# A 3x3 depthwise convolution folded into nine matmuls, or done as one projection matmul and multiply-adds on VectorE

## The chip, the cores and the metric

The kernel runs on one core of a Trainium2 chip. The metric is the device time of one execution in microseconds (us). Engines are named as the profile names them: PE is TensorE (PEld its weight loads), DVE is VectorE, ACT is ScalarE, POOL is GpSimd, SP is SyncE, which here only issues DMAs. ACT issues DMAs too, in order with its other work (ACTq in the profile).

## What is computed

The reference is a stack of four layers on an input of 4 images of 64 x 64 pixels and 96 channels. Layers 0 and 1 are selective scans over the image in four directions; layers 2 and 3 are a linear attention and a quantised feed-forward part. The change is in layers 0 and 1, in the step from the normalised input to the input of the scan:

```python
xz = jnp.einsum('bhwc,ec->bhwe', x, in_proj_w)          # 96 -> 2 x 192 channels
xx, z = jnp.split(xz, 2, axis=-1)
xc = jnp.transpose(xx, (0, 3, 1, 2))
xc = conv_general_dilated(xc, conv_w, (1, 1), [(1, 1), (1, 1)],
                          feature_group_count=E) + conv_b   # 3x3, each of 192 channels by itself
xc = silu(xc)
...
x_dbl = einsum('bkdl,kcd->bkcl', xs, x_proj_weight)     # xs: xc in four orders
delta = softplus(einsum('bkrl,kdr->bkdl', dts, dt_projs_weight) + bias)
... scan over 4096 positions, sum of the four directions, layer norm, * silu(z), out projection
```

x is normalised per group of 3 channels before this.

## The kernel before, in words

The work of layers 0 and 1 is four phases: each of two layers, for each of two pairs of images. `Scans.run` (L701) does for each phase first `prepare` and then `scan_phase`. Beside the `prepare` of a phase runs the `finish` of the phase before it; the last `finish` runs alone. After these come the token layers, which the change doesn't touch.

`prepare` (L151) and `finish` (L548) are Python generators. `run` takes one yield of `prepare` after another, adds the phase's number `beside` to an account at each, and lets `finish` go on by one yield for every full 1.0 in the account (L712). So `beside` says how many yields of `finish` are traced per yield of `prepare`. `finish` has 208 yields. Tracing gives an order of precedence; outside `scan_phase`, which is written under `manual_schedule`, the framework's planner then lays out each engine's queue: it takes, by its own estimate of when inputs and buffers are ready, the earliest traced instruction that is ready. On the chip each engine works through its queue in that fixed order and waits at the head of it. (In the trace, for example, the L277 copies of one half stand between the L270 activations of the other half, which come before them in the code.)

`prepare` does these things in turn:

- loads the small weights and takes the statistics of the two images (L186 to L209), which end in `gs`, the mean and scale per channel;
- loads `in_w` (96 x 192) and the nine taps, broadcast over 96 partitions, and multiplies them into `taps` (96 x 9 x 192) on DVE (L215): nine matrices that hold projection and convolution together;
- `convolve` of image 0 (L220) with `beside` 0.0;
- with `beside` 0.5, `steps` of image 0, 16 calls of 6 yields each with the two in `prepare` itself; in between, `convolve` of image 1 goes on by two yields per call (L228);
- with `beside` 1.7, `steps` of image 1, again 16 calls.

`convolve` (L234) holds the normalised image in `xn`, 66 x 66 with a border of zeros (one buffer). Eight loads of 192 KB on SP's queue (`rawi`, two buffers) bring it, each with every eighth row; DVE normalises each into its strided place (L248). Then, for each half of 96 of the 192 output channels and each of eight chunks of 512 pixels, nine fp32 matmuls accumulate in one of two PSUM banks of the pool `p_c` (L263; the profile shows each as two records), and ACT takes Silu of the bank into `xc` (L270). Last, 16 copies of `xc` scaled on ACT (L277, which reads every eighth float) go to DRAM by DMAs that ACT issues.

`steps` (L285) uses the same two banks. It makes, for a chunk in one direction and for the same chunk in reverse: matmuls (L292), two evacuations on ACT (L295, L296), matmuls (L309), then for each of the two Softplus on ACT (L317), a bf16 copy on ACT (L318), a product on DVE (L319), a difference on DVE (L320), a copy on POOL (L323), a difference on DVE (L324), and DMAs to DRAM that ACT and SP issue (L304, L322, L326). `delta`, `parts` and `du` have two buffers each.

`finish` works through four quarters of the images with single buffers, most of it as one chain over PE, ACT and DVE (L563 to L697), with its loads (`yk`, `ud_f`, `xs`) on SP's queue.

Of the kernel before, what the change touches and what calls it, by code (L numbers as in the profile page):

```python
# [9 lines left out]
F32 = mybir.dt.float32  # L10
# [3 lines left out]
AF = mybir.ActivationFunctionType  # L14
ALU = mybir.AluOpType
# [5 lines left out]
HW = 64  # L21
L = HW * HW
C = 96
E = 192
# [4 lines left out]
PAD = HW + 2  # L29
# [41 lines left out]
def view(t, off, *dims):  # L71

    return bass.AP(t.tensor, t.offset + off, [t.ap[0]] + [list(d) for d in dims])
# [57 lines left out]
class Scans:  # L131
# [19 lines left out]
    def prepare(self, ph):  # L151
# [16 lines left out]
        with self.tc.tile_pool(name="prep", bufs=1) as wp, self.tc.tile_pool(  # L168
# [25 lines left out]
            for i in range(2):  # L194
# [17 lines left out]
            taps = wp.tile([C, 9, E], F32, name="taps")  # L212
            nc.sync.dma_start(taps, a[pre + "conv_w"].unsqueeze(0).broadcast_to([C, 9, E]))

            nc.vector.tensor_tensor(  # L215
                taps, taps, in_w.unsqueeze(1).broadcast_to([C, 9, E]), ALU.mult
            )

            xc = [wp.tile([C, 2, L], F32, name="xc", bufs=2) for _ in range(2)]
            yield from self.convolve(ph, 0, x, xc[0], taps, conv_b, dsum)  # L220
            ph.beside = 0.5
            other = self.convolve(ph, 1, x, xc[1], taps, conv_b, dsum)
            for i in range(2):
                for c in range(NC):
                    for k in range(2):
                        yield from self.steps(ph, sp, xc[i], xp, dt_w, i, k, c)
                        for _ in range(2):
                            next(other, None)  # L228
                            yield
                for _ in other:  # L230
                    yield
                ph.beside = 1.7

    def convolve(self, ph, i, x, xc, taps, conv_b, dsum):  # L234
# [3 lines left out]
        with self.tc.tile_pool(name="conv", bufs=1) as cp:  # L238
            xn = cp.tile([C, PAD, PAD], F32, name="xn")
            for edge in (xn[:, 0, :], xn[:, PAD - 1, :], xn[:, 1 : PAD - 1, 0], xn[:, 1 : PAD - 1, PAD - 1]):  # L240
                nc.vector.memset(edge, 0.0)
            for hl in range(8):
                raw = cp.tile([C, 8, 8, 8], F32, name="rawi", bufs=2)
                nc.sync.dma_start(
                    raw.rearrange("c a h w -> c a (h w)"), x[:, hl * 8 : hl * 8 + 8, i]
                )
                yield
                nc.vector.tensor_scalar(  # L248
                    view(xn, (1 + hl) * PAD + 1, (1, 8), (8 * PAD, 8), (8, 8)),
                    raw,  # L250
                    ph.gs[:, i, 0:1],
                    ph.gs[:, i, 1:2],
                    ALU.subtract,
                    ALU.mult,
                )
            for h in range(2):
                for c in range(NC):
                    if c % 2 == 0:
                        yield
                    ps = self.bank()  # L260
                    for tap in range(9):
                        dy, dx = divmod(tap, 3)
                        nc.tensor.matmul(  # L263
                            rows(ps[:C]),
                            taps[:, tap, h * C : (h + 1) * C],
                            xn[:, ROWS * c + dy : ROWS * (c + 1) + dy, dx : dx + HW],
                            start=tap == 0,
                            stop=tap == 8,
                        )
                    nc.scalar.activation(  # L270
                        xc[:, h, c * TC : (c + 1) * TC], ps[:C], AF.Silu, bias=conv_b[:, h : h + 1]
                    )
            for h in range(2):
                for hl in range(8):
                    yield
# [656 lines left out]
def laid_out(i):  # L932
    x = i["x"].reshape(NP, 2, 8, 8, 8, 8, C)
    a = {"x": x.transpose(0, 6, 3, 5, 1, 2, 4).reshape(NP, C, HW, 2, 64)}
    for n, gamma, beta in (("L0_", "ln_gamma", "ln_beta"), ("L1_", "out_norm_g", "out_norm_b")):
        p = n + "conv_"
        a[n + "in_proj_w"] = i[p + "in_proj_w"].T
        a[n + "conv_w"] = i[p + "conv_w"].reshape(E, 9).T
# [52 lines left out]
```

## Time and profile before

| | us |
|---|---|
| median of 3 runs | 12245.72 |
| lowest and highest run | 12240.04, 12246.47 |
| profiled execution, its own time | 12191.39 |
| span of the profiled execution | 12189.6 |
| L263, the nine taps' matmuls, busy in all | 1033.2 |
| L270, Silu of the convolution, busy in all | 87.3 |
| L248, normalising, 64 instructions, median of one | 0.756 |
| L428, the scans on DVE, busy in all (two groups) | 6347.5 and 868.1 |

The profiled execution was some 54 us shorter than the median of the runs. The page gives, in its second part, the busy share of each engine in 40 slices of the span in tenths; in its fifth part, groups of instructions by line, with busy time, the mean of one and the idle time of the engine ahead of them, with what ended it. A table of stretches gives for each stretch of time the busy time of every engine and, in brackets, its number of instructions, then the granted PE clock as a share of full speed, the busy share of the DMA engines and GB/s.

### The profile page before, as it was taken

The page shows a single profiled execution, that of the slowest core. Times are in us where ns is not written, and L with a number is a line of the kernel's source. Part 1 is how long each engine was busy: PE and PEld are TensorE (multiplying, and loading weights), DVE is VectorE, ACT ScalarE, POOL GpSimd, SP SyncE. Part 2 cuts the span into 40 slices and gives each one's busy share as a digit, 9 for nine tenths or more (in the row PEclk, how much of TensorE's full clock was granted, in tenths as well). Part 3 has the DMA queues.
Part 4 walks back from the last instruction along what each step waited for, and adds up shares of the span by engine and source line. Part 5 has one row for each costly group of instructions (what it writes and reads, how often), then busy time and mean ns, then how long its engine had stood idle before and what let it go on. Part 6 is the DMA issues. An engine that isn't in the chain of part 4 may idle for free.

```text
span 12189.6 us, 340681 instructions
## 1 busy us (share of the span) xinstructions
PE 9338.7 (77%) x147008; PEld 4884.4 (40%) x147008; DVE 9363.7 (77%) x9235; ACT 7063.0 (58%) x11815; POOL 7391.0 (61%) x2316
## 2 busy tenths in 40 slices
PE   7757777769877777769877777768877777776777
PEld 2224444433334444433334444433334444444333
DVE  2479999963569999982569999982459999993667
ACT  2456666643456666653457666653447666662556
POOL 0159999950149999960139999970119999990000
PEclk8669999989779999989778998988778999998887
DMA  3577777744667777754567777764567777773110
GB/s 95 168 228 257 257 254 254 253 167 142 207 211 256 254 254 255 254 199 130 180 217 257 257 258 255 256 215 125 172 201 251 254 254 254 254 249 124 18 21 11
DMA packets 906195, 2491.48 MB, mean 204 GB/s; under 512 B 278030, under 2 KB 560756, under 8 KB 773236
## 3 DMA queue, kind: packets, MB, share of 16 engines
q1 hardware_dynamic: 578036, 2163.43, 52.2%
q10 hardware_dynamic: 326656, 306.25, 8.5%
q8 instruction: 1158, 18.97, 0.7%
q14 instruction: 345, 2.83, 0.1%
HBM read 1955.47 MB, written 513.80 MB: 203 GB/s over the span
## 4 chain that ended last, share of the span: by engine, by line
DMA 57%; PE 20%; SPq 9%; DVE 5%; ACT 4%; issue 3%; POOL 1%; ACTq 1%; DVEq 0%; POOLq 0%
DMA h<-du 52%; SPq L401 9%; PE c L263 8%; PE f L596 2%; PE d L309 2%; DMA yk<-y 1%; PE c L292 1%; DMA delta<-parts 1%; PE f L605 1%; PE f L687 1%; PE f L676 1%; POOL parts L323 1%; DVE parts L324 1%; PE f L662 1%; PE ph L806 1%
## 5 line engine op out<-in xcount | busy, mean ns | idle before, releaser
L411 POOL TENSOR_TENSOR h<-h,b 128x1536 f32<-128x1536 f32 x2048 | 7021.7, 3462 | 527.6 <-DMA h<-du 187.1
L428 DVE TENSOR_TENSOR_SCAN h<-a,carry,h 128x512 f32<-128x512 f32 x5376 | 6347.5, 1259 | 176.7 <-POOL h L411 174.0
L421 ACT ACTIVATE a<-a,a_col 128x512 f32<-128x512 f32 x6144 | 4035.0, 664 | 1869.5 <-PE a L417 1831.7
L446 PEld LDWEIGHTS y<-h,cw 128*32 128x32 f32 x131072 | 2785.2, 128 | 3513.8 <-issue 1328.8
L446 PE MATMUL y<-h,cw 128*32 128x48 f32 x131072 | 3658.5, 266 | 523.3 <-DVE h L428 217.4
L417 PE MATMUL a<-dlt,rep 72*128 72x512 bf16 x6144 | 2529.7, 422 | 1315.1 <-DVE h L428 1228.6
L323 POOL CAST parts<-dl 96x1024 bf16<-96x1024 f32 x256 | 341.2, 1348 | 3092.4 <-DVE dl L320 2708.9
L319 DVE TENSOR_TENSOR du_sb<-dl,xc 96x1024 f32<-96x1024 f32 x256 | 396.2, 1574 | 1292.5 <-ACT dl L317 1241.5
L458 ACT COPY d<-y 128x384 f32<-128x384 f32 x2048 | 979.8, 478 | 468.2 <-PE y L446 418.4
L263 PE MATMUL c<-xn,taps 96*96 96x512 f32 x2304 | 1033.2, 609 | 73.2 <-DVE xn L248 70.8
L428 DVE TENSOR_TENSOR_SCAN h<-a,h 128x512 f32<-128x512 f32 x768 | 868.1, 1200 | 167.5 <-DMA h<-du 69.3
L417 PEld LDWEIGHTS <-rep 72*128 72x128 bf16 x6144 | 486.4, 98 | 829.4 <-issue 566.5
L309 PE MATMUL d<-xd,dt_w 7*96 7x512 f32 x1024 | 518.2, 856 | 255.7 <-ACT xd L295 224.9
L263 PEld LDWEIGHTS c<-xn,taps 96*96 96x96 f32 x2304 | 382.8, 167 | 707.4 <-issue 629.2
L828 POOL MEMSET tn<- 1x4096 f32 x8 | 27.8, 3506 | 861.8 <-PE pa L848 511.9
L270 ACT ACTIVATE xc<-c,conv_b 96x512 f32<-96x512 f32 x128 | 87.3, 682 | 714.3 <-PE c L263 628.2
L596 PE MATMUL f<-yk,perm 128*128 128x384 f32 x1024 | 417.1, 547 | 94.9 <-DMA yk<-y 90.4
L324 DVE TENSOR_TENSOR parts<-dl,parts 96x1024 bf16<-96x1024 f32 x256 | 366.9, 1455 | 154.3 <-POOL parts L323 154.3
L317 ACT ACTIVATE dl<-d 96x1024 f32<-96x1024 f32 x256 | 251.9, 1017 | 392.5 <-DMA delta<-parts 228.2
L292 PE MATMUL c<-xc,x_proj 96*103 96x512 f32 x512 | 421.8, 961 | 4.2 <-ACT xc L270 4.2
L309 PEld LDWEIGHTS d<-xd,dt_w 7*96 7x96 f32 x1024 | 151.9, 212 | 544.6 <-ACT xd L295 296.8
L363 ACT ACTIVATE cw<-c,gmask 128x256 f32<-128x256 f32 x512 | 285.6, 569 | 118.4 <-DMA c<-bc 62.2
(114 smaller groups left out, 5641.4 us busy)
## 6 DMA issues: line engine op xcount, KB each, us to landing
h<-du SPq DMA_DIRECT2D x1024, 768.0 KB
h<-du SPq DMA_DIRECT2D x2048, 384.0 KB
delta<-parts ACTq DMA_DIRECT2D x512, 288.0 KB
dlt<-delta SPq DMA_DIRECT2D x512, 288.0 KB
du<-du_sb SPq DMA_DIRECT2D x256, 384.0 KB
du<-du_sb ACTq DMA_DIRECT2D x256, 384.0 KB
y<-d SPq DMA_DIRECT2D x2048, 48.0 KB
yk<-y SPq DMA_DIRECT2D x256, 384.0 KB
```

The lines of the kernel that those rows point to most:

```text
L263: nc.tensor.matmul(rows(ps[:C]), taps[:, tap, h * C : (h + 1) * C], xn[:, ROWS * c + dy : ROWS * (c + 1) + dy, dx : dx + HW], start=tap == ...
L292: nc.tensor.matmul(rows(ps[:XD2]), xp[:, k, h], u[:, h], start=h == 0, stop=h == 1)
L309: nc.tensor.matmul(ps[:, m], dt_w[part, k, m * C : (m + 1) * C], xd[part], start=True, stop=True)
L324: nc.vector.tensor_tensor(parts[:, 2], delta, parts[:, 1], ALU.subtract)
L401: self.nc.sync.dma_start(u.h[32 * first : 32 * (first + quarters), e : e + n].rearrange("p e t -> p (e t)"), source.rearrange("a g e t -> ...
L411: self.nc.gpsimd.tensor_tensor(h, h, b, ALU.mult)
L417: self.nc.tensor.matmul(u.a[n], self.cst.rep[:, h], u.dl[:, e], start=True, stop=True)
L421: self.nc.scalar.activation(u.a[n], u.a[n], AF.Exp, scale=u.ph.a_col[:, at : at + 1])
L428: self.nc.vector.tensor_tensor_scan(u.h[:, n], u.a.pop(n), u.h[:, n], 0.0 if u.c == 0 else u.ph.carry[:, at : at + 1], ALU.mult, ALU.add,)
L446: self.nc.tensor.matmul(view(u.y[32 * j : 32 * j + 32], l2 * EB, (8 * EB, 4), (1, EB)), u.ph.cw[u.c][:, l1, 8 * j + l2], view(u.h, 64 * l1 ...
L458: self.nc.scalar.copy(u.d[:, :, :, l1], u.y[:, : 32 * EB].rearrange("p (t h x) -> p t h x", t=4, h=2))
L596: nc.tensor.matmul(ps[:, : 4 * C].rearrange("p (w v e) -> p w v e", w=4, v=nv), cst.perm[:, k], view(t, off, (sw if k < 2 else -sw, 4), (1 ...
```

## The change

The projection is done by itself: for each half, eight matmuls with the 96 x 96 half of `in_w` as weights, each on 512 normalised pixels. ACT copies the result out of PSUM into `xp`, the projected half image with its border of zeros (one buffer, used first for one half and then for the other). The input is loaded and normalised once per half, so twice per image, now in place and dense; it is the ACT copy that writes with a stride. The convolution then runs on `xp`: for each chunk of 512 pixels, ACT writes tap 0 times the pixels into the chunk of `xc`, DVE adds the other eight taps with `scalar_tensor_tensor`, in place, each with a scalar per partition, and ACT takes Silu in place. The L277 copies of a half now follow that half.

The weights are no longer multiplied together; the taps are loaded as 96 x 2 x 9. The yields of `convolve` stay 32 per image, but lie otherwise: per half four in the projection, one for each of eight chunks, and four in the copies to DRAM. The numbers `beside` are 1.0 for the convolution of image 0 (with one yield more ahead of it), 0.6 for the steps of image 0 and 1.25 for those of image 1.

```diff
-            taps = wp.tile([C, 9, E], F32, name="taps")
-            nc.sync.dma_start(taps, a[pre + "conv_w"].unsqueeze(0).broadcast_to([C, 9, E]))
-
-            nc.vector.tensor_tensor(
-                taps, taps, in_w.unsqueeze(1).broadcast_to([C, 9, E]), ALU.mult
-            )
+            taps = load("conv_w", [C, 2, 9])
...
-            yield from self.convolve(ph, 0, x, xc[0], taps, conv_b, dsum)
-            ph.beside = 0.5
-            other = self.convolve(ph, 1, x, xc[1], taps, conv_b, dsum)
+            ph.beside = 1.0
+            yield
+            yield from self.convolve(ph, 0, x, xc[0], in_w, taps, conv_b, dsum)
+            ph.beside = 0.6
+            other = self.convolve(ph, 1, x, xc[1], in_w, taps, conv_b, dsum)
...
-                ph.beside = 1.7
+                ph.beside = 1.25
...
             for h in range(2):
+                xp = cp.tile([C, PAD, PAD], F32, name="xp")
+                for edge in (xp[:, 0, :], xp[:, PAD - 1, :], xp[:, 1 : PAD - 1, 0], xp[:, 1 : PAD - 1, PAD - 1]):
+                    nc.vector.memset(edge, 0.0)
+                for hl in range(8):
+                    raw = cp.tile([C, TC], F32, name="rawi", bufs=2)
+                    nc.sync.dma_start(
+                        raw.rearrange("c (a p) -> c a p", p=64), x[:, hl * 8 : hl * 8 + 8, i]
+                    )
+                    if hl % 2 == 0:
+                        yield
+                    nc.vector.tensor_scalar(
+                        raw, raw, ph.gs[:, i, 0:1], ph.gs[:, i, 1:2], ALU.subtract, ALU.mult
+                    )
+                    ps = self.bank()
+                    nc.tensor.matmul(
+                        ps[:C], in_w[:, h * C : (h + 1) * C], raw, start=True, stop=True
+                    )
+                    nc.scalar.copy(
+                        view(xp, (1 + hl) * PAD + 1, (1, 8), (8 * PAD, 8), (8, 8)),
+                        ps[:C].rearrange("c (a h w) -> c a h w", a=8, h=8),
+                    )
                 for c in range(NC):
-                    if c % 2 == 0:
-                        yield
-                    ps = self.bank()
+                    yield
+                    acc = xc[:, h, c * TC : (c + 1) * TC]
                     for tap in range(9):
                         dy, dx = divmod(tap, 3)
-                        nc.tensor.matmul(
-                            rows(ps[:C]),
-                            taps[:, tap, h * C : (h + 1) * C],
-                            xn[:, ROWS * c + dy : ROWS * (c + 1) + dy, dx : dx + HW],
-                            start=tap == 0,
-                            stop=tap == 8,
-                        )
-                    nc.scalar.activation(
-                        xc[:, h, c * TC : (c + 1) * TC], ps[:C], AF.Silu, bias=conv_b[:, h : h + 1]
-                    )
-            for h in range(2):
+                        src = xp[:, ROWS * c + dy : ROWS * (c + 1) + dy, dx : dx + HW]
+                        w = taps[:, h, tap : tap + 1]
+                        if tap == 0:
+                            nc.scalar.activation(rows(acc), src, AF.Copy, scale=w)
+                        else:
+                            nc.vector.scalar_tensor_tensor(
+                                rows(acc), src, w, rows(acc), ALU.mult, ALU.add
+                            )
+                    nc.scalar.activation(acc, acc, AF.Silu, bias=conv_b[:, h : h + 1])
                 for hl in range(8):
-                    yield
+                    if hl % 2 == 0:
+                        yield
```

More of the change, by code (lines that the diff above doesn't have):

```diff
@@ L231, in prepare, with convolve @@
                     yield
-                ph.beside = 1.7
-    def convolve(self, ph, i, x, xc, taps, conv_b, dsum):
+                ph.beside = 1.25
+    def convolve(self, ph, i, x, xc, in_w, taps, conv_b, dsum):
         nc = self.nc
         with self.tc.tile_pool(name="conv", bufs=1) as cp:
[L239 to L245, printed above, removed]
-                )
-                yield
[L248 to L254, printed above, removed]
-                )
-            for h in range(2):
+            for h in range(2):
+                xp = cp.tile([C, PAD, PAD], F32, name="xp")
[19 more added lines that the diff above has]
+                    )
@@ L257, in convolve @@
                 for c in range(NC):
-                    if c % 2 == 0:
-                        yield
-                    ps = self.bank()
+                    yield
+                    acc = xc[:, h, c * TC : (c + 1) * TC]
                     for tap in range(9):
                         dy, dx = divmod(tap, 3)
-                        nc.tensor.matmul(
-                            rows(ps[:C]),
-                            taps[:, tap, h * C : (h + 1) * C],
-                            xn[:, ROWS * c + dy : ROWS * (c + 1) + dy, dx : dx + HW],
-                            start=tap == 0,
-                            stop=tap == 8,
-                        )
@@ L270, in convolve @@
-                    nc.scalar.activation(
-                        xc[:, h, c * TC : (c + 1) * TC], ps[:C], AF.Silu, bias=conv_b[:, h : h + 1]
-                    )
-            for h in range(2):
+                        src = xp[:, ROWS * c + dy : ROWS * (c + 1) + dy, dx : dx + HW]
[6 more added lines that the diff above has]
+                            )
@@ L274, in convolve @@
+                    nc.scalar.activation(acc, acc, AF.Silu, bias=conv_b[:, h : h + 1])
                 for hl in range(8):
-                    yield
+                    if hl % 2 == 0:
+                        yield
                     xu = cp.tile([C, 8, 64], F32, name="xu", bufs=2)
@@ L937, in laid_out @@
         a[n + "in_proj_w"] = i[p + "in_proj_w"].T
-        a[n + "conv_w"] = i[p + "conv_w"].reshape(E, 9).T
+        a[n + "conv_w"] = i[p + "conv_w"].reshape(2, C, 9).transpose(1, 0, 2)
         a[n + "conv_b"] = i[p + "conv_b"].reshape(2, C).T
```

## The prediction

> **What bounds the kernel now.** I read the page first, then the busy time by stretch of the stages outside the scans, then the groups of instructions, the waits and the timelines inside one such stage. The page says that no engine is the bound over the span:
>
> ```profile
> PE 9338.7 (77%) x147008; PEld 4884.4 (40%) x147008; DVE 9363.7 (77%) x9235; ACT 7063.0 (58%) x11815; POOL 7391.0 (61%) x2316
> ...
> DVE  2479999963569999982569999982459999993667
> ```
>
> DVE stands at 9 tenths in four scan phases, which the change doesn't touch, and the dips between them are the four stages that prepare a scan. Only there can time move. Stretches of the first stage (no finish beside it) and of the second; the columns are length, then PE, PEld, DVE, ACT, POOL busy with counts, then PEclk, DMA share, GB/s:
>
> ```profile
> 40.00:178.00 138.00, 126.00 (x287) 47.63 (x288) 5.27 (x8) 20.43 (x24) 0.00 (x0) 1.00 0.10 20
> 178.00:490.00 312.00, 252.62 (x478) 83.62 (x476) 131.75 (x102) 129.96 (x139) 43.09 (x30) 0.74 0.53 152
> 490.00:738.00 248.00, 133.40 (x196) 42.87 (x196) 144.79 (x102) 93.44 (x105) 49.27 (x34) 0.50 0.68 202
> ...
> 2688.00:2816.00 128.00, 128.00 (x293) 48.31 (x293) 2.86 (x4) 21.38 (x25) 0.00 (x0) 0.98 0.08 17
> 2816.00:3140.00 324.00, 284.75 (x671) 111.83 (x670) 143.22 (x150) 147.29 (x170) 39.17 (x28) 0.82 0.59 179
> 3140.00:3525.00 385.00, 316.76 (x959) 166.41 (x958) 223.66 (x318) 180.42 (x236) 43.63 (x36) 0.73 0.65 203
> ```
>
> I call the three stretches A (convolution of image 0 alone), B (steps of image 0, with convolution 1 and some finish) and C (steps of image 1, with the rest of finish). A is PE alone at 100%, 128 us. B is PE at 88%. In C nothing is full. The groups of the second stage (busy, mean ns, idle before):
>
> ```profile
> L263 PE MATMUL c<-xn,taps 96*96 96x512 f32 x576 | 257.5, 607 | 17.9 <-DVE xn L248 17.9
> ...
> L319 DVE TENSOR_TENSOR du_sb<-dl,xc 96x1024 f32<-96x1024 f32 x64 | 99.4, 1576 | 304.2 <-ACT dl L317 287.5 <-DMA du<-du_sb 12.9 <-DMA bc<-xd 3.8
> ...
> L324 DVE TENSOR_TENSOR parts<-dl,parts 96x1024 bf16<-96x1024 f32 x64 | 88.8, 1406 | 41.5 <-POOL parts L323 41.5
> ...
> L277 ACT ACTIVATE xu<-xc,dsum 96x512 f32<-96x512 f32 x32 | 38.5, 1220 | 15.4 <-DMA delta<-parts 6.9 <-DMA ud<-xu 6.8 <-ACT xu L277 0.8
> ```
>
> Without convolution or finish (second image of the first stage) the steps are a serial loop over engines. The DVE timeline there:
>
> ```profile
> 545.62 2.35 DVE L319 TENSOR_TENSOR du_sb<-dl,xc 96x1024 f32<-96x1024 f32 x2 [4.66 <-ACT dl L317]
> 547.90 2.35 DVE L320 TENSOR_TENSOR dl<-dl,parts 96x1024 f32<-96x1024 f32 x2
> 551.18 3.16 DVE L324 TENSOR_TENSOR parts<-dl,parts 96x1024 bf16<-96x1024 f32 x2 [0.93 <-POOL parts L323]
> 559.02 1.92 DVE L319 TENSOR_TENSOR du_sb<-dl,xc 96x1024 f32<-96x1024 f32 x1 [4.68 <-ACT dl L317]
> ```
>
> L319 to L319 is 13.4 us here, and 14.8 for the piece before (530.85 to 545.62). One such round I call a piece, an image has 16: 226 us at this mean, 235 from the stretch of 248 without its first and last half pieces; I take 232 (236 in the first stage). DVE idles some 5.6 us in each, ahead of L319 and L324. Where convolution 1 runs on PE (2920 to 3050), the waits show it standing before the steps, up to 31.3 us at once:
>
> ```profile
> PEld c L263 <- issue: 67.2, 239, 0.8
> DVE du_sb L319 <- ACT dl L317: 61.1, 4, 31.3
> ```
>
> [...] two-input L119 at 96x512 took 677 to 690 ns. [...] table loads took 1283. [...] L324 took 1187 ns at least and up to 2027, beside L323. [...] L277 reads every eighth float and took 1220.
>
> **The change part by part**, for one stage of two images.
>
> PE: 576 records of L263 go (257.5 us); 64 of the same size come (257.5/576 = 0.447, so 28.6). Net -229 us.
>
> DVE: 256 multiply-adds come. The nearest row is L119, 0.684; theirs has a pointer scalar, and the one-column form with one (L203, 215 ns) against the one without (L118, 154) gives 60 ns more: 0.744 us, so 190 us. Bounds: 0.68 without the pointer's price; above, [...] 0.84 for one collision (L324's 2027 less 1187), and GpSimd has 32 casts beside each image's steps, so up to 27 us more. Normalising goes from 16 at 0.753 to 32 dense ones at about 0.54 (L654): 12 to 17. Four memsets become eight per image, 112 ns each: +0.9. The taps product (1.96) goes. Net about +194 us: 97 an image, up to 124 with every collision.
>
> ACT: [...] 32 evacuations with a strided write, between L683's dense 0.582 and L277's strided read 1.22, I take 1.0[...]. Together +55 us. One chunk per yield where there were two can add Silu/Softplus switches: up to 8 pairs of 1.28, 0 to 20 us.
>
> DMA: 16 more loads of 192 KB on SP's queue, 3 MB a stage, 15 us at the 203 GB/s of C; they sit in that queue before finish's yk and xs loads and the steps' du, and each waits for its buffer until a matmul has read it. Hidden by DVE's multiply-adds, except before the first tap. The 648 KB taps load goes.
>
> A. Every tap needs all eight projections, since each covers every eighth row. Loads came in rounds of two, about 3 us (L248 at 2689.6, then 2692.9); now the matmul and the copy add about 1.5: 4 rounds, 18 us. Then 64 x 0.744 = 48 us, then, with one xp buffer, about 15 us of projection before the second half, then 48 us. That is 130 us, against 138 in the first stage and 128 in the second. So A doesn't shrink: DVE takes PE's place. It is 0 in the first stage and I take +10 in the others, where 33 of finish's 208 yields now stand beside it (the last finish, which runs alone, has 107 us of DVE; 33/208 of that is 17, partly in the gaps).
>
> C. Finish has 208 yields; the factor 0.5 over B's 96 yields lets 48 go by, so C has 160. (385-232)/160 = 0.96 us a yield. Now the factors are 1.0 over A's 33 and 0.6 over B's 96, so 208-33-58 = 117 remain: 232 + 112 = 344, so -41.
>
> B. Steps 232, finish 58 x 0.96 = 56, and the part of convolution 1 that isn't hidden. Before, it was 324-232-46 = 46 of 129 on PE, in the first stage 312-236 = 76. DVE has 288-132-30 = 126 us of slack beside steps (half of L319, L320 and L324's 265) and finish (58/208 of 107), and convolution 1 asks for 97 to 124. As DVE serves its queue in order, an L319 behind multiply-adds waits, and ACT's queue now holds a Silu that waits for eight multiply-adds, with Softplus L317 behind it, for which L319 waits. Bounds: nothing exposed, or all 124. I take half of that, 62: the loop's idle is in four places a piece and the multiply-adds come in two bursts. B = 232+56+62 = 350, +26; in the first stage 236+62 = 298, -14.
>
> Sum: 3 x (10+26-41) - 14 = -29 us. Against the profiled execution, 12191.4 (span 12189.6 and 1.8 around it), this makes 12162. That execution lies 54 us under the runs' median; the difference carried to the median gives 12217.
>
> **The rivals.**
> *DVE and ACT lock step (slower).* Place: B. The multiply-adds of two chunks, 16 x 0.744 = 12 us, meet a loop with 5.6 us of slack, and ACT, with 147 us busy and 5.2 us of DMA issue a piece (L322, L326 and L304 in its timeline; 83 us), gets 28 to 48 more. For it: every DVE operation of the loop is on its path. Against: only 8 of B's 16 pieces get multiply-adds. If 105 instead of 62 is exposed in each of the four stages, that is +172, so +143: 12389. It is slower than before from about 69 exposed.
> *PE was the drag (faster).* PE is 82% busy in C and 88% in B. If C follows PE's load (43 of finish's 208 yields leave it, 55 of its 267 us of PE, so 262 of 317 remain: 318 us, -67) and B exposes only a quarter of 124 (31, so 319, -5; first stage -45): 3 x (10-5-67) - 45 = -231: 12015. For it: the 31.3 us wait. Against: the loop alone, in the first stage's C, leaves PE half idle and takes its 232 all the same.
> *The change doesn't move the stages*, because the planner's order hides either work: 12246. Little speaks for it, A being fully exposed.
>
> **How the numbers follow.** Forecast 0.50 (spread some 60 us either way), lock step 0.30, PE drag 0.18, no movement 0.02. 0.2% is 24 us, about what a measurement of this kernel tells from no change. Faster by more: 0.25 of the forecast's 0.50 and 0.18, 0.43. Within: 0.15 + 0.02 = 0.17. Slower: 0.10 + 0.30 = 0.40. Both signs are likely; the forecast's own range is 12140 to 12295. The whole one goes to 12050, which leaves out over half of the fast rival (0.11), and to 12430, which leaves out a third of lock step (0.09), where all 124 and some table loads are exposed.
>
> **What would show it.** A: DVE over 70% busy in a stretch of 125 to 145 us, PE under 45%. Multiply-adds of 0.72 to 0.78 us[...]. B near 350 us: over 390 is lock step, with waits of L317 behind Silu and of Silu for DVE; under 325 is PE drag. C near 344. The prediction is wrong if A itself grows past 150 us, through gaps before each half, or if finish is left over after C.

## The result and the profile after

The changed kernel took 12214.17 us (median of 19 runs) against 12240.04 us of the kernel before (19 runs beside it): a ratio of 0.9981, 95% interval 0.9973 to 0.9990. So it is some 23 us faster, at the edge of what this kernel's measurement can tell. The forecast of 12217 us is met. But its parts, one for each stretch of a stage, are not: all three failed and their errors cancelled, which is what this study is about.

The page after, its lines of busy time and of DVE's slices:

```profile
PE 8693.3 (71%) x144960; PEld 4628.3 (38%) x144960; DVE 10072.3 (82%) x10351; ACT 7378.4 (60%) x12140; POOL 7390.2 (60%) x2316
...
DVE  6679999987669999987669999997559999993667
```

PE is down by 645 us over the span, DVE up by 709, ACT up by 315. In the dips between the scan phases DVE's slices of 2 to 6 tenths have become 5 to 8. The work went over to DVE, as announced, and the time hardly moved.

The profiled executions can't be subtracted as they stand: their spans are 12189.6 us before and 12223.4 after, because the four scan phases, whose code is the same, took 44 us more in the second one (7466 against 7421 us; a phase lay anywhere between 1836 and 1878 us in the profiles of this study). I therefore measure each stage alone, from the end of the last scan to the first one of the next phase. A ends with the 16th Silu of the convolution, B with the 32nd L323 (L324 before), C with the 64th. The time for statistics and small weights, some 40 us, is in A here. Each kernel's stages are read from one profiled execution. Its three later stages, which do the same work, differ among themselves by up to 2.6 us in A, 9 in B and 10 in C, so a difference of a few us between two means says little in B or C.

| us | A | B | C | whole stage |
|---|---|---|---|---|
| before, first stage | 179.5 | 330.6 | 228.1 | 774.0 |
| after, first stage | 169.3 | 331.2 | 234.4 | 771.0 |
| before, mean of the other three | 188.4 | 358.7 | 349.4 | 930.7 |
| after, mean of the other three | 187.5 | 362.7 | 341.2 | 926.7 |

The four stages sum to 3566 us before and 3551 after: 15 us less, of which A gives 13, C 18, and B and the way to the scan take 16 back. The stretches of the second stage (A, B, C) before, in the columns of the prediction's table:

```profile
2625.60:2814.90 189.30, 135.15 (x554) 55.22 (x555) 26.15 (x53) 29.97 (x39) 0.00 (x0) 0.84 0.19 46
2814.90:3171.30 356.40, 308.96 (x727) 122.83 (x725) 160.83 (x163) 163.38 (x187) 44.96 (x32) 0.80 0.58 177
3171.30:3518.10 346.80, 293.65 (x904) 155.91 (x904) 206.01 (x305) 165.40 (x219) 37.84 (x32) 0.75 0.66 208
```

and after, with B and C of the first stage ahead of them:

```profile
169.30:500.50 331.20, 158.34 (x220) 44.68 (x220) 229.05 (x248) 168.41 (x179) 43.02 (x32) 0.58 0.56 158
500.50:734.90 234.40, 124.76 (x184) 40.19 (x184) 135.78 (x96) 89.41 (x100) 46.43 (x32) 0.50 0.69 200
2641.70:2829.10 187.40, 86.31 (x492) 46.23 (x492) 123.11 (x224) 76.50 (x101) 0.00 (x0) 0.67 0.40 113
2829.10:3192.20 363.10, 231.59 (x468) 96.03 (x468) 253.77 (x326) 192.44 (x219) 45.42 (x32) 0.59 0.59 169
3192.20:3533.20 341.00, 260.30 (x712) 130.65 (x712) 191.38 (x252) 168.14 (x208) 38.01 (x32) 0.70 0.62 187
```

B went from PE at 87% to PE at 64% and DVE at 70%, and it is no shorter. Two things are to be seen against the prediction. B ends at 3171 in the profile before, not at 3140, where I had cut it. And the first stage's B is 331 us in both kernels, to within 1 us. The groups after, over the whole second stage:

```profile
L268 DVE SCALAR_TENSOR_TENSOR xc<-xp,conv_w,xc 96x512 f32<-96x512 f32 x256 | 176.5, 746 | 4.9 <-ACT xc L266 3.5 <-ACT xp L254 0.4
L308 PE MATMUL d<-xd,dt_w 7*96 7x512 f32 x256 | 141.7, 926 | 54.3 <-ACT xd L294 49.5 <-ACT xd L295 4.7
L251 PE MATMUL c<-rawi,in_w 96*96 96x512 f32 x64 | 53.9, 952 | 47.5 <-DVE rawi L247 38.7 <-ACT xp L254 7.0 <-issue 0.9
L254 ACT COPY xp<-c 96x512 f32<-96x512 f32 x32 | 34.9, 1111 | 27.3 <-PE c L251 14.9 <-DMA du<-du_sb 5.3 <-DVE parts L323 2.7
L266 ACT ACTIVATE xc<-xp,conv_w 96x512 f32<-96x512 f32 x32 | 21.4, 714 | 17.0 <-DVE du_sb L318 9.3 <-DVE xc L268 6.4 <-DMA bc<-xd 1.1
```

A multiply-add's record is 0.746 us long, as worked out, and DVE hardly idles ahead of them (4.9 us in all). But in a row the records overlap: 256 of them keep DVE busy for 176.5 us, 0.69 each, not for 190. In the first stage, where nothing else stands beside them, a row of 64 takes 42.5 us, 0.664 each:

```profile
126.01 42.48 DVE L268 SCALAR_TENSOR_TENSOR xc<-xp,conv_w,xc 96x512 f32<-96x512 f32 x64 [3.76 <-ACT xc L266]
```

The projection's 64 records keep PE busy for 53.9 us, nearly twice what I had carried over from the nine taps.

A of the second stage in its four pieces (first loads and projection, first half's taps, second half's projection, second half's taps):

```profile
2684.00:2707.00 23.00, 19.49 (x61) 10.32 (x62) 5.04 (x14) 9.75 (x13) 0.00 (x0) 0.81 0.72 205
2707.00:2757.00 50.00, 26.84 (x104) 16.76 (x103) 44.90 (x69) 18.87 (x30) 0.00 (x0) 0.84 0.58 172
2757.00:2779.00 22.00, 13.77 (x16) 2.92 (x15) 10.87 (x45) 19.80 (x21) 0.00 (x0) 0.50 0.57 126
2779.00:2830.00 51.00, 18.57 (x53) 9.02 (x51) 50.97 (x72) 23.79 (x31) 0.39 (x1) 0.60 0.05 15
```

The prediction had 18, 48, 15 and 48 for these; with some of finish's work beside them they are 23, 50, 22 and 51. In the first stage, without finish, DVE's timeline gives 20, 44, 22 and 42: the rows of multiply-adds are shorter than predicted and the projections longer, and the sum is the same. In both tap pieces DVE is the bound (90% and 100%), and PE is busy for 54% and 36%. Over the 146 us DVE is busy for 112, 77%, where the prediction asked for over 70% in 125 to 145; PE, with 54%, is above the 45% that it named, by finish's matmuls (in A of the first stage, without them, it is 30%).

### The profile page after: what moved, and what is told of

Same layout as the page of the kernel before. It is cut to its first block, busy times and chain, and to the rows that moved or that the text cites. A ratio compares the mean times of both kernels' runs of the same rounds, so it can differ in the third digit from the quotient of the medians.

```text
span 12223.4 us, 338353 instructions
## 1 busy us (share of the span) xinstructions
PE 8693.3 (71%) x144960; PEld 4628.3 (38%) x144960; DVE 10072.3 (82%) x10351; ACT 7378.4 (60%) x12140; POOL 7390.2 (60%) x2316
## 5 line engine op out<-in xcount | busy, mean ns | idle before, releaser
L308 PE MATMUL d<-xd,dt_w 7*96 7x512 f32 x1024 | 576.7, 960 | 372.4 <-ACT xd L294 360.8
L268 DVE SCALAR_TENSOR_TENSOR xc<-xp,conv_w,xc 96x512 f32<-96x512 f32 x1024 | 707.0, 750 | 33.9 <-ACT xc L266 28.7
L595 PE MATMUL f<-yk,perm 128*128 128x384 f32 x1024 | 464.3, 600 | 133.1 <-DMA yk<-y 89.7
L323 DVE TENSOR_TENSOR parts<-dl,parts 96x1024 bf16<-96x1024 f32 x256 | 350.2, 1383 | 170.3 <-POOL parts L322 167.9
L308 PEld LDWEIGHTS d<-xd,dt_w 7*96 7x96 f32 x1024 | 174.1, 235 | 694.2 <-ACT xd L294 447.4
L251 PE MATMUL c<-rawi,in_w 96*96 96x512 f32 x256 | 220.1, 974 | 261.0 <-DVE rawi L247 166.3
L319 DVE TENSOR_TENSOR dl<-dl,parts 96x1024 f32<-96x1024 f32 x256 | 307.7, 1218 | 63.6 <-ACT parts L317 62.2
```

What stands on the lines that cost most here:

```text
L268: nc.vector.scalar_tensor_tensor(rows(acc), src, w, rows(acc), ALU.mult, ALU.add)
L308: nc.tensor.matmul(ps[:, m], dt_w[part, k, m * C : (m + 1) * C], xd[part], start=True, stop=True)
L323: nc.vector.tensor_tensor(parts[:, 2], delta, parts[:, 1], ALU.subtract)
L595: nc.tensor.matmul(ps[:, : 4 * C].rearrange("p (w v e) -> p w v e", w=4, v=nv), cst.perm[:, k], view(t, off, (sw if k < 2 else -sw, 4), (1 ...
```

## The experiments

The change does two things at once: it moves the convolution, and it deals finish's yields out anew (0.0, 0.5, 1.7 became 1.0, 0.6, 1.25). The table gives the means of stages two to four, and the ratio to the kernel before with its interval where there are enough runs. The first four rows, the next four and the last four were each measured beside runs of before of their own. In three kernels (marked as a single run) part of the work is left out altogether.

| kernel | A | B | C | stage | first stage | ratio |
|---|---|---|---|---|---|---|
| new convolution alone | 177.5 | 353.3 | 355.5 | 921.0 | 772.2 | 0.9967 (0.9955 to 0.9980) |
| new shares alone | 204.3 | 401.5 | 335.8 | 976.3 | 772.2 | 1.0086 (1.0069 to 1.0103) |
| after, fewer multiply-adds | 187.8 | 339.7 | 337.2 | 899.1 | 746.4 | single run |
| before, fewer tap matmuls | 188.0 | 329.0 | 352.0 | 903.6 | 730.8 | single run |
| second xp | 177.7 | 354.7 | 355.8 | 922.6 | 771.1 | 0.9974 (0.9961 to 0.9986) |
| A split between PE and DVE | 134.2 | 369.6 | 357.9 | 895.9 | 731.5 | 0.9858 (0.9833 to 0.9883) |
| first tap on DVE | 179.3 | 353.0 | 355.8 | 922.9 | 770.1 | 0.9965 (0.9952 to 0.9979) |
| and evacuation on DVE | 179.0 | 352.0 | 356.2 | 921.3 | 767.9 | 0.9966 (0.9955 to 0.9978) |
| no convolution 1 | 176.7 | 286.5 | 358.5 | 856.1 | 686.1 | single run |
| yields into A alone | 187.9 | 360.5 | 350.0 | 933.7 | 770.6 | 0.9996 (0.9988 to 1.0005) |
| fewer yields in B | 177.5 | 343.3 | 381.3 | 938.1 | 772.8 | 1.0016 (1.0008 to 1.0025) |
| A split, fewer yields in B | 134.0 | 355.9 | 382.2 | 907.4 | 730.6 | 0.9887 (0.9872 to 0.9903) |

**The two halves of the change.** The new convolution with the old shares, and the old convolution with the new shares:

```diff
 new convolution alone, against after
-            ph.beside = 1.0
-            yield
-            ph.beside = 0.6
+            ph.beside = 0.5
-                ph.beside = 1.25
+                ph.beside = 1.7
 new shares alone, against before: the same lines the other way round
```

> The changed kernel with the shares of finish as they were (0.0 beside convolution 0, 0.5 and 1.7 beside the steps, no extra yield). Theory: the convolution is as long on VectorE as it was on TensorE, in A and in B, and the small gain comes from the 33 yields of finish that lie free beside A. Then nothing is gained here: 12225 to 12260 us, A 10 us shorter than in the changed kernel at most, C back at 347 to 353. Rival (the move of the convolution itself earns the gain, the shares earn nothing): 12205 to 12220.

> The kernel before with the new shares of finish alone (1.0, 0.6, 1.25 and the extra yield); the convolution stays on TensorE. Theory: TensorE is full in A, so 33 yields of finish there lengthen A by their own TensorE time, 267 x 33/208 = 42 us in three stages, and C gives back no more than the 6 to 11 us that it lost in the changed kernel: about 12240 + 3 x 33 = 12340 us. Rival (the shares alone earn the gain): 12215 or less.

The first is faster than before, at 0.9967; the second slower, at 1.0086. My theory for the first falls: not the shares earn the gain, the convolution does, and it earns all of it. (The interval of its ratio overlaps with that of the whole change; but three more kernels below, with the new convolution, the old shares and a small edit of their own, lie at 0.9965 to 0.9974, and the stages say the same.) For the second kernel the theory had the time nearly right, 100 us more where 108 were measured, but not the place: it put 42 us a stage into A and nothing into B. Stretches of the second stage, the convolution alone:

```profile
2629.40:2807.00 177.60, 51.83 (x314) 17.95 (x314) 108.89 (x187) 66.50 (x81) 0.00 (x0) 0.53 0.21 51
2807.00:3159.60 352.60, 207.47 (x450) 87.05 (x450) 251.82 (x309) 184.70 (x212) 48.30 (x32) 0.62 0.62 183
3159.60:3515.40 355.80, 300.45 (x908) 157.44 (x908) 206.57 (x306) 170.62 (x224) 37.87 (x32) 0.75 0.66 205
```

A is 11 us shorter than before, B 5, C 6 longer (four of the copies to DRAM of image 1, which ACT makes and issues, now fall into it). Against this kernel the shares of the change add 10 us to A and 9 to B and take 14 from C: they cost 6 us a stage. With the old convolution it is worse; its A and B:

```profile
2632.30:2836.50 204.20, 161.61 (x680) 74.42 (x681) 32.63 (x81) 37.66 (x52) 0.00 (x0) 0.88 0.31 93
2836.50:3239.50 403.00, 326.11 (x794) 137.48 (x793) 170.88 (x189) 172.76 (x201) 46.38 (x32) 0.78 0.52 154
```

On the mean A is 16 us and B 43 us longer than before. My reading is that finish meets a PE there that is nearly full (before, it was busy for 87% of B); no run separates this from the order of the work. So the cost of shares depends on where the convolution runs, and the two edits belong together. The gain in C, 14 us, is the same with either convolution.

**How much of the taps is exposed in B.** Both kernels with most taps of image 1 left out. After, seven of its eight multiply-adds per chunk are left out; before, seven of nine matmuls. I had put this at 84 us of DVE and 100 us of PE a stage. In B of the first and the second stage DVE's busy time fell by 75 and 75 us, PE's by 79 and 94:

```diff
 after
-                    for tap in range(9):
+                    for tap in range(9 if i == 0 else 2):
 before: the same, with stop at the last tap that is left
```

> The changed kernel with seven of the eight multiply-adds left out for image 1 of each pair, so the second image's convolution has only its first two taps: 16 x 7 x 0.750 = 84 us of VectorE go from B in each stage. Theory (fully exposed): B is 75 to 90 us shorter in each stage, in all about 11880 us. The prediction's half hidden: B 42 us shorter, 12045 us. Hidden: no change.

> The kernel before with seven of nine tap matmuls left out for image 1 of each pair: 16 x 7 x 2 x 0.447 = 100 us of TensorE go from B in each stage. Theory (as exposed on TensorE as on VectorE): B is 75 to 100 us shorter, in all about 11880 us. The prediction's share (46 of 129 exposed with finish beside): B 36 us shorter, about 12080 us.

B falls by 27 us in the first stage and by 23 in the others without the multiply-adds, by 42 and 30 without the matmuls. The prediction had half of the multiply-adds exposed; measured on DVE's 75 us it is a third. Of PE's taps half was exposed in the first stage (42 of 79) and a third in the others (30 of 94), near the 36 us that the prediction's share gave. So for the taps alone, a change of engine wins some 7 to 15 us a stage in B, although it takes 129 us of tap matmuls from the busiest engine there; first tap, evacuation and the second loading come on top.

**The gap between the two halves.** In A the second half's projection stands between the two rows of multiply-adds. To give it a second buffer, the xp of that half is laid into the memory of the other image's xc, which isn't used yet (in A alone, on top of the new convolution alone):

```diff
-                xp = cp.tile([C, PAD, PAD], F32, name="xp")
+                if h == 1 and spare is not None:
+                    xp = view(spare, 0, (PAD, PAD), (1, PAD))
+                else:
+                    xp = cp.tile([C, PAD, PAD], F32, name="xp")
```

> As the convolution alone with the old shares of finish (40 us under the kernel before), but in A the projected second half goes into memory of its own (the output buffer of image 1, not in use yet), so that its projection need not wait for the last multiply-add of the first half. Theory: the one xp buffer costs A a gap of about 20 us between the halves, in each stage; A 15 to 20 us shorter, in all 100 to 120 us under the kernel before. Rival (A is bound by the multiply-adds and what must stand in their queue, the gap only moves): A within 5 us, 40 us under the kernel before.

A stays at 177.7 against 177.5. My theory that the buffer makes the gap falls; DVE's timeline shows why (line numbers of that kernel: L248 normalises, L269 is the multiply-add):

```profile
2703.11 41.47 DVE L269 SCALAR_TENSOR_TENSOR xc<-xp,conv_w,xc 96x512 f32<-96x512 f32 x62 [1.87 <-ACT xc L267]
2744.50 0.54 DVE L248 TENSOR_SCALAR rawi<-rawi,gs 96x512 f32<-96x512 f32 x1
...
2746.08 0.74 DVE L269 SCALAR_TENSOR_TENSOR xc<-xp,conv_w,xc 96x512 f32<-96x512 f32 x1
2749.78 0.54 DVE L248 TENSOR_SCALAR rawi<-rawi,gs 96x512 f32<-96x512 f32 x1 [2.96 <-DMA rawi<-in_x]
...
2756.77 0.54 DVE L248 TENSOR_SCALAR rawi<-rawi,gs 96x512 f32<-96x512 f32 x1 [4.09 <-PE c L252]
...
2769.30 6.04 DVE L269 SCALAR_TENSOR_TENSOR xc<-xc,conv_w 96x512 f32<-96x512 f32 x9 [3.76 <-ACT xc L267]
```

The memory is free, but the second half's normalising stands in DVE's queue behind the first half's multiply-adds, 62 of which run before it (in the changed kernel, the first two loads of the second half are issued at 2716.65 and 2717.35 us and normalised at 2754.52 and 2755.64, after 60 multiply-adds in a row of 39.93 us and without a wait of DVE's); then a load, a matmul and a copy per eighth follow one after the other until 2769.30. The free buffer didn't help here, since the work that would use it stood behind other work in its own queue.

**Where convolution 1's time lies.** From the convolution alone, the first tap of image 1 goes to DVE, then the evacuation too. ACT's busy time in B falls by 9 us with the first; with both it falls by 31 in the first stage and by 22 in the second:

```diff
-                        if tap == 0:
+                        if tap == 0 and i == 1:
+                            nc.vector.tensor_scalar_mul(rows(acc), src, w)
+                        elif tap == 0:
 second kernel, on top
-                    nc.scalar.copy(
+                    copy = nc.vector.tensor_copy if i == 1 else nc.scalar.copy
+                    copy(
```

> As the convolution alone with the old shares, but the first tap of image 1 is a product on VectorE in place of ScalarE: 11 us of ScalarE less and some 9 of VectorE more in B of each stage. Theory after the left-out taps (B's exposed part is what ScalarE's queue holds, VectorE's is hidden to two thirds): B 8 to 20 us shorter, 70 to 120 us under the kernel before. Rival (VectorE's queue is what B waits for): B 3 to 9 us longer, 5 to 30 us under.

> As the one before, and the evacuation of image 1's projection is on VectorE as well: 29 us of ScalarE less in all and about 21 of VectorE more in B. Theory (ScalarE's queue): B 20 to 40 us shorter than with the convolution alone, 120 to 200 us under the kernel before. Rival (VectorE's queue): B 7 to 20 us longer, 40 us over to 10 us under the kernel before.

B's mean goes from 353.3 to 353.0 and 352.0, in the first stage from 332.4 to 329.0 and 328.4. Neither theory decides: B follows neither ACT's queue nor DVE's. A kernel without convolution 1, in which a memset stands for each chunk of xc and the copies to DRAM remain, says how much there is in all:

```diff
                 for hl in range(8):
+                    if i == 1:
+                        if hl % 2 == 0:
+                            yield
+                        continue
...
+                    if i == 1:
+                        nc.vector.memset(acc, 0.25)
+                        continue
                     for tap in range(9):
```

> The convolution of image 1 is left out except for its yields, the memsets of xp's border and the 16 xu copies with their DMAs; a DVE memset writes each chunk of xc. So B of the first stage holds only the steps, 16 xu copies of each image and the way into the first piece. With the convolution it was 332 us, without seven of its eight multiply-adds 304, and C is 235. Theory (what is left of B over C is loads, projection, evacuation and Silu of convolution 1): B of the first stage falls to 250 to 268 us, that is C plus some 20 us until the first Softplus. Rival (it is the xu copies, whose DMAs ACT issues, and the start, which all versions have): B stays at 285 to 300, and no placement of the convolution would have won B more than 35 to 45 us.

B and C of its first stage, and B of its second:

```profile
168.10:414.00 245.90, 122.73 (x182) 38.97 (x182) 135.87 (x104) 106.46 (x114) 46.49 (x32) 1.00 0.70 199
414.00:649.60 235.60, 123.50 (x184) 39.71 (x184) 135.84 (x96) 87.05 (x98) 46.37 (x32) 1.00 0.69 200
2734.60:3018.20 283.60, 181.69 (x418) 77.85 (x418) 159.11 (x163) 123.78 (x145) 45.23 (x32) 0.63 0.70 212
```

B falls to 246 us, 10 over C, a little below the theory's 250: it is the convolution, not the start or the copies. So convolution 1 costs B 332 - 246 = 86 us in the first stage and 353 - 286 = 67 in the others. Leaving out seven of eight multiply-adds alone took 27 and 23 of that. The larger rest comes with loads, normalising, projection, evacuation, first tap and Silu, which count on either engine: 22 to 31 us of them moved between two engines changed B by 4 us at most. (What the multiply-adds would cost with that rest gone was not measured.) Against the same 246, the convolution on PE cost the first stage 331 - 246 = 85. The 246 are those of the new kernel, though: there the first L324 of B (L323 after) ends 15 to 18 us after A, in the kernel before 30 us after it, so of the 85 up to 12 us may be a later start of the steps (the part on the split shows why). These runs show the amount; what holds the loop up is not shown.

**What a yield of finish is worth.** Two kernels with the new convolution and other shares: 33 yields from C into A, or 24 from B into C.

```diff
 yields into A alone, against the new convolution alone
+            ph.beside = 1.0
+            yield
-                ph.beside = 1.7
+                ph.beside = 1.35
 fewer yields in B
-            ph.beside = 0.5
+            ph.beside = 0.25
-                ph.beside = 1.7
+                ph.beside = 2.0
```

> The new convolution with finish's shares 1.0 in A (33 yields, one more yield ahead of it), 0.5 in B and 1.35 in C: against the new convolution with the old shares only 33 of finish's yields go from C to A, and B keeps its 48. Theory (a yield is worth about 0.33 us in C and costs 0.3 in A): A +10, B within 4, C -11 in each of the three later stages, in all the ratio of the convolution alone, 0.9967 (0.995 to 0.9985). Rival (a yield in C is worth its average, (350-235)/160 = 0.72 us): C -24, the sum -14 a stage, ratio 0.9925 to 0.994. If B grows by 8 or more although its share is the same, it is the order, not the number of yields, that costs B.

> The new convolution with finish's shares 0.0 in A, 0.25 in B (24 yields) and 2.0 in C: against the old shares, 24 yields go from B to C. Theory (10 more yields of finish made B 7 to 11 us longer, so one costs B about 1 us and is worth 0.33 in C): B -20 to -26, C +8 in each of three stages, ratio to before 0.991 to 0.9945. Rival (B is set by its steps and convolution, and finish lies in their gaps): B within 5 of 353, C +8 to +17, ratio 0.998 to 1.001.

No single price fits: in the first run A grew by 10 us as expected, but both theories fail on C, which falls by 5.5 us (theory -11, rival -24); so do both of the second, where it rises by 26 (theory +8, rival up to +17). C of the two kernels, in the second stage:

```profile
3188.70:3539.00 350.30, 260.20 (x732) 134.62 (x730) 192.29 (x257) 162.52 (x205) 36.62 (x32) 0.70 0.60 182
```

```profile
3161.50:3543.60 382.10, 320.25 (x1000) 172.91 (x1000) 221.75 (x325) 182.43 (x243) 41.54 (x32) 0.74 0.62 191
```

Put in order of finish's yields, C's prices come out one by one. Yields 24 to 47: (381.3 - 355.5)/24 = 1.07 us each. Yields 48 to 80: (355.5 - 350.0)/33 = 0.17. Yields 81 to 90: (350.0 - 341.2)/10 = 0.88. The 117 that are left in after: (341.2 - 235)/117 = 0.91. The code fits this in part: each quarter of finish has 52 yields, 18 that gather (loads and matmuls, L563 to L611) and 34 in the chain of layer norm, gate and projection. 24 to 47 and 81 to 90 are chain alone, 48 to 80 hold the 18 that gather of the second quarter. But 33 yields with 15 of the chain at 1 us would cost 15 us, not 5.5, so this is not the whole of it, and it is argued from the code. In B the 24 cost 10 us, 0.42 each, less than half of what they cost in C. That B grew by 7 us with its 48 yields unchanged, but 33 later in finish, no run explains.

**A split over both engines.** In A one engine is nearly idle or half idle while the other is full: before, PE is busy for all of the prediction's window of 128 us and DVE for 2.9 us of it; after, DVE is busy for 90% and 100% of the two tap pieces and PE for 54% and 36%. So image 0's channels 0 to 95 are projected and convolved on DVE as in the change, channels 96 to 191 with nine matmuls on PE as before, side by side, on top of the new convolution alone:

```diff
-            yield from self.convolve(ph, 0, x, xc[0], in_w, taps, conv_b, dsum)
+            yield from self.convolve_split(ph, 0, x, xc[0], xc[1], in_w, fused, taps, conv_b, dsum)
...
+                        nc.vector.scalar_tensor_tensor(
+                            rows(acc), src, w, rows(acc), ALU.mult, ALU.add
+                        )
...
+                    nc.tensor.matmul(
+                        rows(ps[:C]),
+                        fused[:, tap],
+                        xn[:, ROWS * c + dy : ROWS * (c + 1) + dy, dx : dx + HW],
```

> As the convolution alone with the old shares, but in A the two engines share image 0: output channels 0 to 95 by projection and multiply-adds on VectorE, channels 96 to 191 by the nine fused matmuls on TensorE. Theory: A is as long as one engine's work on it, with the other idle, so sharing makes A about 12 + 7 + 62 = 81 us after the statistics in place of 130: A 45 to 60 us shorter in each stage, 220 to 280 us under the kernel before. Rival (planner's order and evacuations on ScalarE make one wait for the other): A 20 us shorter, 120 us under.

A and B of its second stage:

```profile
2597.70:2731.80 134.10, 81.23 (x427) 34.34 (x428) 64.27 (x116) 39.75 (x56) 0.00 (x0) 0.78 0.22 54
2731.80:3100.90 369.10, 218.04 (x467) 88.62 (x465) 251.84 (x309) 194.46 (x221) 45.75 (x32) 0.62 0.60 176
```

A falls by 42 us in the first stage and by 43 in the others, just under the low end of what was expected; B grows by 4 in the first stage and by 16 in the others. The traces show where: in the start of B. With the convolution alone, DVE is busy for 108.9 us of A's 177.6 and PE for 51.8, and PE and ACT do the first step beside the second half's multiply-adds, Softplus included, before A ends at 2807.0:

```profile
2777.41 4.43 PE L306 MATMUL d<-xd,dt_w 7*96 7x512 f32 x8 [0.77 <-ACT xd L292]
2781.17 1.93 ACT L314 ACTIVATE dl<-d 96x1024 f32<-96x1024 f32 x2 [1.12 <-PE d L306]
```

In the split kernel PE is busy with taps until A's end (2731.8), and the first step's matmuls come behind them:

```profile
2714.56 16.47 PE L340 MATMUL c<-xc,fused 96*96 96x512 f32 x38
2730.87 1.88 PE L372 MATMUL c<-xc,x_proj 96*103 96x512 f32 x4
2744.33 1.02 ACT L397 ACTIVATE dl<-d 96x1024 f32<-96x1024 f32 x1
```

The kernel before has the same order, with A's end at 2814.9:

```profile
2814.06 5.30 PE L292 MATMUL c<-xc,x_proj 96*103 96x512 f32 x8
2827.21 1.02 ACT L317 ACTIVATE dl<-d 96x1024 f32<-96x1024 f32 x1
```

So the split kernel's first L404 (L324 before) ends 31 to 32 us after A in the later stages, near the 30 of the kernel before, against 18 with the convolution alone: that is 13 to 14 of the 16 us. In the first stage the start is as late, but 8 of its 12 us are made up again; why is not settled. The ratio of 0.9858 (0.9833 to 0.9883) beats both kernels. With fewer yields of finish in B it does worse:

> The convolution of image 0 split between PE and DVE, with the shares 0.0, 0.25 and 2.0 in place of 0.0, 0.5 and 1.7. Theory (one yield costs about 1 us in B and 0.33 in C): B falls from 368 to 371 by 20 to 26, C rises from 356 to 359 by 8, so the ratio to before goes from 0.986 to 0.981 to 0.983. Rival (finish lies in B's gaps): B within 5, C +8 to +17, ratio 0.988 to 0.990.

B falls by 14, C rises by 24, the ratio is 0.9887. The theory falls, and the rival is right in the sum, though not in its parts: B falls by more than its 5, and C rises by more than its 17. It fits the last part, where the chain's yields are dearer in C than in B. That points the other way, to more yields in B and none in A; this wasn't tried.

## Why the prediction was right, and where it was wrong

The number was right: 12217 forecast, 12214.17 measured, and the sign too. But the hit is luck: the working was right in some terms and held in sum only because the others erred in opposite directions by some 100 us.

- **Engine times on DVE and ACT: single records right, sums off.** The multiply-add was put at 0.744 us and took 0.750 on the mean of all 1024; but in a row they overlap (0.664 to 0.69 each), so DVE took on 177 us a stage, not 194. A delay beside a POOL copy, as 76 of the 256 L324 had before (2.02 to 2.03 us, each begun while an L323 ran; the other 180 took 1.19 to 1.22), came 11 times in 1024: these took 1.41 to 1.52 us, each begun while a POOL copy ran (24 more overlapped with a copy that began after they had, and took 0.735 to 0.744). Two multiply-adds, the second of them delayed, and the copy:

```profile
271.28 2.18 DVE L268 SCALAR_TENSOR_TENSOR xc<-xp,conv_w,xc 96x512 f32<-96x512 f32 x2
271.48 1.44 POOL L322 CAST parts<-dl 96x1024 bf16<-96x1024 f32 x1 [20.97 <-DVE dl L319]
```

  The first tap took 0.714 us (its share of the +55 was my estimate, which no trace of before showed), the evacuation 1.111 (put at 1.0, between 0.582 and 1.22). ACT took on 79 us a stage, not 55: there are 69 more table loads of 1.283 us in the four stages, 22 us a stage, a little above the upper end of what was allowed for them.
- **PE's relief: mis-sized, without effect.** "576 records go, 64 of the same size come": they took 53.9 us, not 28.6. PE's busy time in the second stage fell from 738 to 578 us, by 160, not 229. Outside A, where the whole convolution left PE anyway, little hung on it.
- **A, "0 in the first stage, +10 in the others": failed.** The 130 us that I worked out are right in sum, though not in their pieces: A of the first stage ended at 169.3, 129 us after its start at 40. But the same stretch before ended at 179.5, so 140, and my own 138 against 130 would have given -8; I charged 0. For the second stage I took the 128 us from a window that was cut when PE was already full. The move gained 10 to 11 us in every stage (169.0 and 177.5 against 179.5 and 188.4), and the 33 yields of finish, whose +10 was right, took it back in the three later ones.
- **B, "half of 124 exposed": the total nearly right, its content wrong.** Convolution 1, measured with the old shares, costs B 67 us in the later stages, near my 62, and 86 in the first. But of the multiply-adds only a third is exposed, and most is work that I hadn't priced there: the rest of the convolution. The loop of the steps takes 246 in B, not 232 or 236. And the step failed as a difference: I put "-14" in the first stage because PE's convolution seemed to cost 76 of 312 there, where B had been cut 20 us short (real: 85 of 331). That the first step starts 12 to 15 us earlier when PE is free in A had no term at all. The true change is +0.6, and in the others +4 in place of +26, since the earlier B was 359, not 324.
- **C, "(385-232)/160 = 0.96 us a yield", -41: the term that failed most.** Measured -8 against before, -14 at equal convolution: 0.33 for each of the 43 yields. The smaller part of the error is the boundary: C was 349 us, not 385, which makes the average (349 - 228)/160 = 0.76, and -33 in place of -41. The larger part, from -33 to -14, is that an average was used as a marginal price: the yields that the change took out are among the cheapest of all, 0.17 for 33 of them.
- **The rivals.** Lock step asked for 105 us of convolution 1 to be exposed through its multiply-adds. These account for 23 to 27 us, a quarter of that. The 86 us of the first stage lie beyond the 69 from which lock step decides by itself, and yet nothing is lost there, because the old convolution cost 85. PE as the drag fell in C: in the second stage PE's work there went down to 260 us, as that rival had it (262), and C stayed at 341, not 318. In B it holds for the 30 to 42 us by which PE's taps were exposed, and DVE's share took their place. Both treat one engine as the bound of a loop in which no engine is full (in B after, PE 64% and DVE 70%).

In the sum, over four stages: A came 43 us better than predicted and B 51 better, C 105 worse, and the way to the scan 4 worse. From -29 that makes -14, and the stages measure -15.

## What to carry to other kernels

When work that was spread over a serial loop changes engine, take the work out of the kernel first and see how much of it is exposed: here some 85 us of 331 in B's first stage on either engine (on PE perhaps 12 less, by the later start), which bounds any gain before a line is written. Where two engines take turns at being full in a stretch that stands alone, the gain lies in giving each half of the work, not in moving it all from one to the other: against before, the split made A 54 us and the whole later stage 35 us shorter, the move 11 and 10. Of the 43 us that the split won in A against the move, it lost 16 in B, mostly because the engine that had been free in A no longer did B's first step meanwhile; so ask first what a free engine does in its free time. Before a share or a schedule is priced with "so many us per step", check that the steps are alike, and cut stretches by an instruction that ends them, not by a round time.

## What was unexpected of the hardware

The records of other matmuls became longer, though nothing about them was changed: L308 (L309 before) from 814 to 926 ns over the second stage. Before:

```profile
L309 PE MATMUL d<-xd,dt_w 7*96 7x512 f32 x256 | 127.1, 814 | 30.3 <-ACT xd L295 24.9 <-ACT xd L296 5.4
```

Each half of the change does it alone: the same matmul with the new convolution alone, with the new shares alone, and in the kernel before with seven of nine of image 1's taps left out:

```profile
L306 PE MATMUL d<-xd,dt_w 7*96 7x512 f32 x256 | 137.0, 888 | 66.3 <-ACT xd L292 56.7 <-ACT xd L293 6.4 <-ACT dl L314 3.3
L311 PE MATMUL d<-xd,dt_w 7*96 7x512 f32 x256 | 137.6, 889 | 69.7 <-ACT xd L297 66.3 <-ACT xd L298 3.4
L310 PE MATMUL d<-xd,dt_w 7*96 7x512 f32 x256 | 121.1, 811 | 64.0 <-ACT xd L296 58.1 <-ACT xd L297 5.9
```

So it is not simply that the taps left PE: in the third kernel most taps are gone from B, and the records stay as they were.

The records are not equally long everywhere: those of 512 columns took 603 ns in the full stream of the taps (L263, 126.4 us without a gap in before), and 1082 ns in C of the first stage, where PE is busy for 53% of the time (1083 there before, too); what makes up the difference, these runs don't separate. How busy PE is does not settle it: in the third kernel above PE was busy for only 65% of its B, and over the stage its records took 811 ns. What decides between 811 and 926 ns stays open; the effect is that PE's busy time fell by 645 us where 916 (four times 229) had been predicted. Some 100 us of the difference are the projection (53.9 in place of 28.6 us a stage), the rest, by subtraction, are longer records of work that was left alone. The column PEclk doesn't go with the durations either. In C of the first stage it shows 0.50 after and 1.00 in the kernel without convolution 1, and the same matmul takes the same time in both:

```profile
L308 PE MATMUL d<-xd,dt_w 7*96 7x512 f32 x128 | 73.4, 1082 | 105.5 <-ACT xd L294 105.5
```

```profile
L313 PE MATMUL d<-xd,dt_w 7*96 7x512 f32 x128 | 72.2, 1084 | 103.5 <-ACT xd L299 102.5 <-ACT xd L300 1.1
```
